# Convolution tiles kept as sums and differences of neighbours along the width, between three global convolutions and a Haar layer

## The chip, the cores and the metric

One core of one Trainium2 chip runs the whole program. The metric is device time in microseconds, the median of several runs. The core has a matrix engine (TensorE, in profiles PE, with its weight loads as PEld), a vector engine (VectorE, DVE), an activation engine (ScalarE, ACT), GpSimd (POOL) and a queue engine (SyncE, SP). The engines run side by side, each takes its own instructions in order, and they meet through semaphores. SBUF is the working memory with 128 partitions, PSUM the memory that matmuls write, DRAM the memory outside; DMA queues, here issued by SP and ACT, move data between DRAM and SBUF.

## What is computed

The input x has 4 images of 64 channels of 256 x 256, all in float32. Four layers follow each other:

```python
x = conv(x, L0); x = conv(x, L1); x = haar_mix(x, L2); x = conv(x, L3)

def conv(x, ...):                      # once per layer, filters hx, hy [256, 64] from a small network
    k = hx[:, None, :] * hy[None, :, :]            # separable kernel of channel c
    y = causal_2d_convolution(x, k)                # along height and width, cut to 256 x 256
    return y + x * bias[:, None, None]

def haar_mix(x, v, conv_w, tau):
    f1 = haar2d(x)                                 # full Haar transform along width and height
    f4 = einsum('bchw,oc->bohw', f1 * v[i], conv_w[i])          # for i = 0, 1, summed after
    f5 = sign(f4) * relu(abs(f4) - tau[i])                      # the soft threshold
    return haar2d_inverse(sum of f5) + x
```

The convolution is separable and causal, so the kernel does it as two products with Toeplitz matrices, one along the height and one along the width. The first step of the Haar transform along the width takes the sum and the difference of each pair of neighbouring columns, and the last step of the inverse makes the pair out of sum and difference again.

## The kernel before, in words

**A tile** is one channel of one image, 128 partitions x 2 x 256: row p of the upper and of the lower half. `toeplitz` (L249) loads a tile t of 128 x 2 x 256 from a short padded filter row in DRAM (`pads`), with overlapping reads: t[:, 0] is the band along the height, t[:, 1] the one along the width. `contract` (L258) is one product: four matmuls, each of which the page counts as two records. `first` (L264) multiplies a tile with the height band (PSUM tile pa) and ScalarE copies the product to SBUF (a, L275); this leaves it transposed. `second` (L279) multiplies a with the width band (PSUM tile py), which puts it back, and VectorE adds tile times bias (L292) into the result.

**Stages.** For each image b: `convolutions` (L322) loads x and runs layers 0 and 1 for each channel: stages load, a0, y0, a1, y1. Stage pairs (L335) then makes the sums and differences of neighbours of y1 with two VectorE operations, into the rings sums (4 channels) and sd (8 channels), and keep stores both in DRAM. Further levels of the width transform follow on VectorE and POOL (L344), two fp32r copies of the result (ACT L369, VectorE L374), the transform along the height as one matmul with a Haar matrix (pz, L381), and a store (coef). `mixing` (L425) runs 64 groups: load f, matmul with the channel weights (px, L449), scale (VectorE L468 and ACT L473), size and sign (ACT L477, L480), threshold and product (VectorE L484, L488), and a sum into the large tile z (L494). `inverse` (L517) takes z back: levels in place (VectorE L299, L300), copy of a channel (ACT L534), matmuls pw (L541, L542), for the first 16 channels a further product pu (L548 to L555), and join (L560): r, which is the kept sums and differences, times 0.5 plus the PSUM result gives t (L563), and two more operations (L566, L567) make neighbours out of its sums and differences, tile u. Then layer 3 runs on u (stages a3, y3) and the result is stored (out). For the first three images every third channel is put off: its u goes to DRAM (late), and `convolution` (L614) runs layer 3 on it beside the mixing of the last image.

**Order.** Every stage of every unit gets a time in ticks: the start of its unit plus an entry of `PLACE` (L26). The events are sorted by it (L680) and emitted in this order, and the tile framework sets the order of the instructions on each engine from it, places tiles into buffers and puts in all waits. A tick of the mixing is one group with, for images 1 to 3, about 0.9 channels of convolution; a tick of the inverse is one channel. Tiles come from rings by tag: y (5 buffers) holds y0 and u, in (3) holds x and the reloaded u, res (1) holds y1 and t, co (3) holds the result of layer 3 and the coefficients before their store; the six buffers of toep hold Toeplitz tiles.

**Start.** `filters` (L169) computes the filters of each layer from the small network on 128 partitions (64 for the height, 64 for the width) and stores them with `end` (L206) into pads, one store on ACT's queue, one on SP's; the first Toeplitz load waits for both. Dummy matmuls (`occupy`, L161) run on TensorE meanwhile.

Of the kernel before, what the change touches and what calls it, by code (L numbers as in the profile page):

```python
# [9 lines left out]
F32 = mybir.dt.float32  # L10
F32R = mybir.dt.float32r
AF = mybir.ActivationFunctionType
ALU = mybir.AluOpType
# [3 lines left out]
B, C, S, EMB, ORD = 4, 64, 256, 33, 64  # L17
P = 128
ROW = S + P

GT = 4
BUFS = {"res": 1, "y": 5, "co": 3}

N_ACT = (12, 12, 12, 8)

PLACE = {  # L26
    "load": 0.714,
    "a0": 1.643,
    "a0 copy": 1.643,
    "y0": 2.571,  # L30
# [2 lines left out]
    "a1 copy": 3.5,  # L33
    "y1": 4.429,
    "y1 sum": 4.429,
    "pairs": 4.639,
    "keep": 4.929,
    "levels": 0.73,
    "split": 0.734,
# [22 lines left out]
    "a3 copy": 2.471,  # L62
    "y3": 3.542,
    "y3 sum": 3.542,
    "out": 4.537,
    "level": 0.6,
    "l load": 0.316,
    "l a3": 1.855,
    "l a3 copy": 1.855,
    "l y3": 2.783,  # L70
    "l y3 sum": 2.783,
    "l out": 4.4,
    "l mix load": -0.977,
    "l mix": 0.21,
    "l scaled": 0.583,
# [22 lines left out]
def conv_seq_kernel(ctx, tc, x, fz, fw, bias, decay, haar, haar_row, factors, vt, taut, wmix, out):  # L98
# [14 lines left out]
    nc = tc.nc  # L113
# [27 lines left out]
    keep = [dram.tile([C, P, 2, 2, P], F32, name=f"keep{b}") for b in range(B)]  # L141
    coef = [dram.tile([2, C, P, S], F32, name=f"coef{b}") for b in range(B)]
    scales = dram.tile([S // 4 // GT, P, 2, GT, 16], F32, name="scales")
    pads = [dram.tile([C, 2, ROW], F32, name=f"pad{layer}") for layer in range(3)]
    late = dram.tile([B, C, P, 2, S], F32, name="late")


# [21 lines left out]
    def filters(layer, queue, done, behind=None):  # L169

        fz_sb, fw_sb = part(S + P, EMB), part(3 * P + 4)
        fb = part(3)
        par = 3 * P
        st = {}

        def load():
            nc.sync.dma_start(fz_sb, fz[layer])
            queue.dma_start(fw_sb, fw[layer])

            nc.vector.tensor_scalar(fb, fw_sb[:, par : par + 3], fw_sb[:, par + 3 : par + 4], None, ALU.mult)  # L180

        def begin(n):
            ps = bank(f"fp{layer}_{n}").rearrange("p m s -> p (m s)")[:, :S]
            if n == 0:
                nc.tensor.matmul(ps, fz_sb[:, S:], fz_sb[:, :S], start=True, stop=True)
            else:
                nc.tensor.matmul(ps, fw_sb[:, (n - 1) * P : n * P], st["h"], start=True, stop=True)
            u, k = st["u"], st["k"] = part(S), part(S)
            nc.scalar.activation(u, ps, AF.Identity, bias=fb[:, n : n + 1], scale=fw_sb[:, par + 3 : par + 4])

            first = nc.vector.tensor_scalar(k, u, INV_2PI, MAGIC, ALU.mult, ALU.add)
            if behind is not None:
                tc.add_manual_dep(first.ins, behind[n].ins.name, order, reason="the first layer goes first")
            nc.vector.tensor_scalar(k, k, -MAGIC, None, ALU.add)

        def finish(n):
            u, k, h = st["u"], st["k"], part(S)
            for c in (C1, C2):
                step = nc.vector.scalar_tensor_tensor(u, k, -c, u, ALU.mult, ALU.add)
                if n == 2 and behind is not None:  # L200
                    tc.add_manual_dep(step.ins, behind["out"].ins.name, order, reason="the first layer goes first")
            done[n] = nc.vector.tensor_scalar(u, u, PI_IN, -PI_IN, ALU.min, ALU.max)
            nc.scalar.activation(h, u, AF.Sin)
            st["h"] = h

        def end():  # L206
            ps = bank(f"fo{layer}").rearrange("p m s -> p (m s)")[:, :S]
            nc.tensor.matmul(ps, fw_sb[:, 2 * P : 3 * P], st["h"], start=True, stop=True)
            f = part(ROW)
            nc.vector.memset(f[:, S:], 0.0)  # L210
            done["out"] = nc.vector.scalar_tensor_tensor(f[:, :S], ps, dsb[:, S:], dsb[:, :S], ALU.mult, ALU.mult)
            for axis, queue in enumerate((nc.scalar, nc.sync)):
                queue.dma_start(pads[layer][:, axis, :], f[axis * C : (axis + 1) * C])
            st["f"] = f

        steps = [(lambda n=n, do=do: do(n)) for n in range(3) for do in (begin, finish)]
        return [load, *steps, end]
# [31 lines left out]
    def toeplitz(layer, c, name):  # L249

        t = tp.tile([P, 2, S], F32, name=name, tag="toep")
        nc.sync.dma_start(t, ap(pads[layer], c * 2 * ROW, [[1, P], [ROW, 2], [1, S]]))
        return t

    def bank(name):
        return psm.tile([P, 2, S], F32, name=name, tag="mm")

    def contract(ps, src, t):  # L258

# [19 lines left out]
    def second(b, st, key, layer, res, new, tag, ahead=None):  # L279


        def product(c):
            s = st[c]
            if ahead is not None:
                s[ahead] = toeplitz(ahead, c, f"t{ahead}_{b}_{c}")
            s["p" + new] = bank(f"p{new}_{b}_{c}")
            contract(s["p" + new], s[key], s[layer][:, 1, :])

        def residual(c):
            s = st[c]  # L290
            y = io.tile([P, 2, S], F32, name=f"{new}_{b}_{c}", tag=tag, bufs=BUFS[tag])
            nc.vector.scalar_tensor_tensor(y, s[res], bsb[:, layer, c : c + 1], s["p" + new], ALU.mult, ALU.add)  # L292
            s[new] = y

        return [product, residual]

    def halve(even, odd):

        nc.vector.tensor_sub(odd, even, odd)  # L299
        nc.vector.scalar_tensor_tensor(even, even, 2.0, odd, ALU.mult, ALU.subtract)  # L300

    def level(n, chunk, begin=0, count=None):

        count = n if count is None else count
        v = z.rearrange("p n s x c -> p n s (x c)")[:, chunk].rearrange("p (j e s) x -> p j e s x", e=2, s=P // 2 // n)
        halve(v[:, begin : begin + count, 0, 0, :], v[:, begin : begin + count, 1, 0, :])

    def butterfly():

# [12 lines left out]
    def convolutions(b, ticks, in_parts=(), border=None):  # L322


        st = {}
# [2 lines left out]
            return tick if border is None or tick < border or n < C // 4 - 2 else border + 3 * (tick - border)  # L328

        def load(c):  # L330
            xt = io.tile([P, 2, S], F32, name=f"x_{b}_{c}", tag="in", bufs=3)
            nc.sync.dma_start(xt, x[b, c].rearrange("(k p) w -> p k w", p=P))
            st[c] = {"x": xt, 0: toeplitz(0, c, f"t0_{b}_{c}")}

        def pairs(c):  # L335
            v = st.pop(c)["y1"].rearrange("p k (w e) -> p k w e", e=2)
            nc.vector.tensor_add(sums[:, c % 4], v[:, :, :, 0], v[:, :, :, 1])
            nc.vector.tensor_sub(sd[:, c % 8, 1], v[:, :, :, 0], v[:, :, :, 1])

        def store(c):  # L340
            nc.sync.dma_start(keep[b][c, :, 0], sums[:, c % 4])
# [48 lines left out]
        def away(c):  # L390
# [3 lines left out]
            nc.sync.dma_start(coef[b][:, c].rearrange("k p w -> p k w"), t)  # L394

        work = zip(
            ("load", "a0", "a0 copy", "y0", "y0 sum", "a1", "a1 copy", "y1", "y1 sum", "pairs", "keep"),
            [
                load,
                *first(b, st, "x", 0, "a0"),  # L400
                *second(b, st, "a0", 0, "x", "y0", "y", ahead=1),
                *first(b, st, "y0", 1, "a1"),
                *second(b, st, "a1", 1, "y0", "y1", "res"),
                pairs,
                store,
            ],
        )
# [109 lines left out]
    def inverse(b, start, put_off):  # L517
# [41 lines left out]

        def join(c):  # L560
            ps = st[c]["pw"]
            t = io.tile([P, 2, 2, P], F32, name=f"t_{b}_{c}", tag="res", bufs=BUFS["res"])
            nc.vector.scalar_tensor_tensor(t, st[c]["r"], 0.5, ps, ALU.mult, ALU.add)  # L563
            u = io.tile([P, 2, S], F32, name=f"u_{b}_{c}", tag="y", bufs=BUFS["y"])
            v = u.rearrange("p m (w e) -> p m w e", e=2)
            nc.vector.tensor_add(v[:, :, :, 0], t[:, 0], t[:, 1])  # L566
            nc.vector.tensor_sub(v[:, :, :, 1], t[:, 0], t[:, 1])  # L567
            st[c]["u"] = u

        def aside(c):  # L570
            nc.scalar.dma_start(late[b, c], st.pop(c)["u"])
# [17 lines left out]
        for c in range(C):  # L589
# [8 lines left out]
            if c in put_off:  # L598
                at(turn + PLACE["aside"], aside, c)
            else:  # L600
                shift = (0.0, 0.0)
                if put_off:
                    shift = ((-0.27, -0.342), (0.23, 0.158))[c % 3]
                for name, stage in zip(("a3", "a3 copy", "y3", "y3 sum", "out"), last(b, st)):
                    at(turn + PLACE[name] + shift[name[0] != "a"], stage, c)

    def last(b, st, queue=nc.scalar):
        return [
            *first(b, st, "u", 2, "a3"),
            *second(b, st, "a3", 2, "u", "y3", "co"),  # L610
            lambda c: queue.dma_start(out[b, c].rearrange("(k p) w -> p k w", p=P), st.pop(c)["y3"]),
        ]

    def convolution(which, ticks):  # L614

        for (b, c), tick in zip(which, ticks):
            st = {}

            def load(c, b=b, st=st):
                u = io.tile([P, 2, S], F32, name=f"v_{b}_{c}", tag="in", bufs=3)  # L620
                nc.sync.dma_start(u, late[b, c])
                st[c] = {"u": u, 2: toeplitz(2, c, f"t2_{b}_{c}")}

            for name, stage in zip(("l load", "l a3", "l a3 copy", "l y3", "l y3 sum", "l out"), [load, *last(b, st, nc.sync)]):
                at(tick + PLACE[name], stage, c)
# [168 lines left out]
```

## Time and profile before

| | |
|---|---|
| median of 3 runs | 2874.51 us (2872.78 to 2877.79) |
| profiled execution, its own time | 2874.07 us |
| its span, first to last instruction | 2872.3 us |
| granted TensorE clock, mean | 0.999 |
| ScalarE, VectorE and POOL busy, first row of their kind | ACT 72%, DVE 87%, POOL 12% |
| DMA, mean over the span | 226 GB/s |
| Toeplitz loads (t<-pad) | 768 of 256 KB, 4.1 us from issue to landing |
| x loads | 256 of 256 KB, 3.7 us |
| result stores from ACT's queue | 193 of 256 KB, 4.3 us |

The first matmul of a convolution starts at 25.17 us, after the filters. The stages of the span, read from the rows of each: convolutions of image 0 alone until about 420 us; mixing of image 0 with convolutions of image 1 until 840; the inverse of image 0 until 1080; the same pair for image 1 (mixing until 1500, inverse until 1740) and image 2 (2160, 2340); mixing of image 3 beside the channels that were put off until about 2640; the inverse of image 3 until the end.

Rows of instructions are read like this: line of the program, engine, operation, output<-inputs, output shape<-input shape, and how often. The times of a timeline row are its start and its duration. A duration is longer than what the instruction takes from its engine, since the next one starts before it ends; so a cost is read from start to start where the engine has no gap.

### The profile page before, as it was taken

What the parts mean: (1) busy time and instruction counts of PE and PEld (TensorE: products, weight loads), DVE (VectorE), ACT (ScalarE), POOL (GpSimd) and SP (SyncE); (2) the same over time, 40 slices, a digit from 0 to 9 for tenths busy, and PEclk for the clock granted to TensorE, in tenths of its full rate; (3) what the DMA queues carried; (4) which work ended last, traced back from release to release, by engine and by line L of the source; (5) the groups of instructions that cost most, each with busy time, mean ns of one, the idle gap of its engine ahead of it and who ended that gap; (6) DMA issues with size and microseconds to landing.
All of it is one profiled execution on the core that took longest, in us unless ns stands there. A gap on an engine that the chain in (4) does not pass through costs nothing. (4 is left out here: it accounts for less than half of the span.)

```text
span 2872.3 us, 52434 instructions
## 1 busy us (share of the span) xinstructions
PE 2827.1 (98%) x16592; PEld 2555.6 (89%) x16592; DVE 2494.9 (87%) x4255; ACT 2080.3 (72%) x4950; POOL 334.4 (12%) x644
## 2 busy tenths in 40 slices
PE   9999999999999999999999999999999999999999
PEld 7899998898888898998898998998898998888998
DVE  4655558999999779999999779999999779999985
ACT  2333338999995558998985658999995659998554
POOL 0111111121121001221221001121121000000000
PEclk9999999999999999999999999999999999999999
DMA  6878787776667986777777986777777988787786
GB/s 182 249 231 230 232 232 227 207 208 204 205 209 213 289 254 198 214 213 214 209 207 236 299 255 196 213 214 216 208 208 235 297 266 235 229 238 212 224 241 201
DMA packets 599367, 649.77 MB, mean 226 GB/s; under 512 B 48465, under 2 KB 517044, under 8 KB 598964
## 3 DMA queue, kind: packets, MB, share of 16 engines
q1 hardware_dynamic: 536996, 578.61, 68.9%
q10 hardware_dynamic: 62096, 67.82, 6.7%
q8 instruction: 134, 2.20, 0.3%
q14 instruction: 141, 1.16, 0.1%
HBM read 426.77 MB, written 219.48 MB: 225 GB/s over the span
## 5 line engine op out<-in xcount | busy, mean ns | idle before, releaser
L261 PE MATMUL py<-t,a 128*128 128x256 f32 x3072 | 922.5, 382 | 9.5 <-ACT a L275 8.7
L275 ACT COPY a<-pa 128x512 f32<-128x512 f32 x768 | 478.8, 623 | 498.6 <-PE pa L262 455.2
L473 ACT ACTIVATE f<-px,vt 128x64 f32<-128x64 f32 x2816 | 610.5, 367 | 101.6 <-DVE f L468 101.1
L262 PEld LDWEIGHTS py<-t,a 128*128 128x128 f32 x3072 | 583.4, 190 | 79.3
L262 PE MATMUL py<-t,a 128*128 128x128 f32 x3072 | 590.0, 274 | 0.0
L261 PEld LDWEIGHTS py<-t,a 128*128 128x128 f32 x3072 | 497.3, 191 | 51.2 <-ACT a L275 19.0
L449 PE MATMUL px<-wb,f 128*128 128x256 f32 x2048 | 487.6, 380 | 7.6 <-ACT f L473 7.6
L449 PEld LDWEIGHTS px<-wb,f 128*128 128x128 f32 x2048 | 369.0, 190 | 50.0 <-ACT f L473 10.5
L351 POOL TENSOR_TENSOR sd<-less 128x128 f32<-128x128 f32 (+4 forms) x320 | 190.8, 596 | 1858.7 <-DVE less L350 1519.9
L534 ACT COPY zc<-z 128x512 f32<-128x512 f32 x256 | 282.1, 1105 | 108.1 <-PE pw L542 99.0
L484 DVE TENSOR_TENSOR mag<-mag,vt 128x1024 f32<-128x1024 f32 x256 | 316.6, 1237 | 12.3 <-ACT mag L477 11.5
L488 DVE SCALAR_TENSOR_TENSOR mag<-mag,f 128x1024 f32<-128x1024 f32 x256 | 316.6, 1238 | 0.0
L261 PE MATMUL pa<-t,y 128*128 128x256 f32 x1024 | 309.1, 384 | 6.8 <-DVE y L292 5.2
L261 PE MATMUL pa<-t,x 128*128 128x256 f32 x1024 | 305.9, 381 | 0.5 <-DMA t<-pad 0.5
L477 ACT ACTIVATE mag<-f 128x1024 f32<-128x1024 f32 x256 | 295.7, 1155 | 2.8 <-DVE z L494 0.4
L374 DVE TENSOR_TENSOR sp<-sd,sp 128x512 fp32r<-128x512 f32 x256 | 179.8, 702 | 129.3 <-ACT sp L369 128.2
L480 ACT ACTIVATE f<-f 128x1024 f32<-128x1024 f32 x256 | 285.8, 1116 | 3.5
L261 PE MATMUL pa<-t,u 128*128 128x256 f32 x772 | 233.2, 384 | 6.5 <-ACT w L548 2.8
L292 DVE SCALAR_TENSOR_TENSOR y<-x,bsb,py 128x512 f32<-128x512 f32 x256 | 190.9, 746 | 41.9 <-PE py L262 41.0
L262 PEld LDWEIGHTS pa<-t,x 128*128 128x128 f32 x1024 | 194.6, 190 | 26.3
L262 PEld LDWEIGHTS pa<-t,y 128*128 128x128 f32 x1024 | 194.5, 190 | 26.3
L292 DVE SCALAR_TENSOR_TENSOR y<-y,bsb,py 128x512 f32<-128x512 f32 x256 | 190.7, 745 | 26.0 <-PE py L262 25.6
(73 smaller groups left out, 4412.3 us busy)
## 6 DMA issues: line engine op xcount, KB each, us to landing
t<-pad SPq DMA_DIRECT2D x768, 256.0 KB, 4.1
x<-in_x SPq DMA_DIRECT2D x256, 256.0 KB, 3.7
coef<-co SPq DMA_DIRECT2D x256, 256.0 KB, 3.2
f<-coef SPq DMA_DIRECT2D x256, 256.0 KB, 3.2
r<-keep SPq DMA_DIRECT2D x256, 256.0 KB, 4.1
out_y<-y ACTq DMA_DIRECT2D x193, 256.0 KB, 4.3
keep<-sums SPq DMA_DIRECT2D x256, 128.0 KB, 2.8
keep<-sd SPq DMA_DIRECT2D x256, 128.0 KB, 2.8
```

What stands on the lines that cost most here:

```text
L261: nc.tensor.matmul(ps[:, m, :], src[:, 0, m * P : (m + 1) * P], t[:, ::-1], start=True, stop=False)
L262: nc.tensor.matmul(ps[:, m, P:], src[:, 1, m * P : (m + 1) * P], t[:, : P - 1 : -1], start=False, stop=True)
L275: nc.scalar.copy(a, s["p" + new])
L292: nc.vector.scalar_tensor_tensor(y, s[res], bsb[:, layer, c : c + 1], s["p" + new], ALU.mult, ALU.add)
L351: engine.tensor_tensor(t[:, :, :, half:length], v[..., 0], v[..., 1], ALU.subtract)
L449: nc.tensor.matmul(ps[:, q, h, :], f[:, q, h * P : (h + 1) * P], wb.rearrange("p r n -> p (r n)"), start=True, stop=True,)
L473: nc.scalar.mul(f4[:, j], px[:, j], scale(g, 0)[:, j : j + 1])
L477: nc.scalar.activation(mag, st[g]["f4"], AF.Abs)
L480: nc.scalar.activation(st[g]["f4"], st[g]["f4"], AF.Sign)
L484: nc.vector.tensor_sub(mag, mag, over(g, 1, 16))
L488: nc.vector.scalar_tensor_tensor(mag, mag, 0.0, st[g]["f4"], ALU.max, ALU.mult)
L534: nc.scalar.copy(a.rearrange("p h k i -> p (h k) i"), z[:, c // 16, :, :, c % 16].rearrange("p i x -> p x i"))
```

## The change

Tiles of layers 0, 1 and 3 are kept in another form along the width: in place of columns 2n and 2n + 1 they hold their sum and their difference, alternating. The width band is brought into this form too, so that a product with it takes alternating sums and differences to alternating sums and differences. The height products are as they were.

- x is turned into this form by two POOL operations of 128 x 256 (`butterflies`, stage pairs, now between load and the Toeplitz load, which is a stage of its own, bands). The x load moves from 0.714 to -1.0 ticks.
- y1 needs no tile of its own and no pairs after it: its residual is two VectorE operations of half a tile that write straight into sums and sd.
- join makes u with two VectorE operations of half a tile out of r and the PSUM result. Channels that are put off still get plain neighbours, by the three operations of before, since their layer 3 runs on plain tiles with plain bands (pads[3]).
- After layer 3 a new stage, neighbours, turns the result back with two POOL operations (two VectorE ones for the very last channel), and out, which stores it, moves from 4.537 to 5.2. The late channels' store (l out) moves from 4.4 to 4.8.
- `end` stores four padded rows per channel in place of two: the height filter twice, once shifted by one, and two width rows in the new form, which six short VectorE operations on 64 partitions make. A Toeplitz load reads them with three levels: 64 steps of two elements, 4 rows, 256 elements. The first two channels of each image load height and width bands separately (EARLY).
- The rings in and res are gone, y has nine buffers.

```diff
-BUFS = {"res": 1, "y": 5, "co": 3}
+BUFS = {"y": 9, "co": 3}
...
-            for axis, queue in enumerate((nc.scalar, nc.sync)):
-                queue.dma_start(pads[layer][:, axis, :], f[axis * C : (axis + 1) * C])
+            for i, queue in enumerate((nc.sync, nc.scalar)):
+                queue.dma_start(pads[layer][:, i, 0, : ROW - 1], f[:C, i : i + ROW - 1])
+            g0, g1, g2 = (f[C:, i : i + S : 2] for i in range(3))
...
+            nc.vector.tensor_add(sums, g0, g2)
+            nc.vector.tensor_sub(less, g0, g2)
+            nc.vector.scalar_tensor_tensor(w[:, 0, :P, 1], sums, 0.5, g1, ALU.mult, ALU.add)
+            nc.vector.tensor_scalar(w[:, 0, :P, 0], less, -0.5, None, ALU.mult)
+            nc.vector.tensor_scalar(w[:, 1, :P, 1], less, 0.5, None, ALU.mult)
+            nc.vector.scalar_tensor_tensor(w[:, 1, :P, 0], sums, -0.5, g1, ALU.mult, ALU.add)
+            nc.sync.dma_start(pads[layer][:, :, 1, :], w.rearrange("p i n o -> p i (n o)"))
...
-        nc.sync.dma_start(t, ap(pads[layer], c * 2 * ROW, [[1, P], [ROW, 2], [1, S]]))
+        if layer == 0 and c < EARLY:
+            for axis in range(2):
+                nc.sync.dma_start(
+                    t[:, axis], ap(pads[layer], (c * 4 + axis) * ROW, [[2, P // 2], [2 * ROW, 2], [1, S]])
+                )
+        else:
+            nc.sync.dma_start(t, ap(pads[layer], c * 4 * ROW, [[2, P // 2], [ROW, 4], [1, S]]))
...
+    def butterflies(engine, t, name):
+
+        new = io.tile([P, 2, S], F32, name=name, tag="y", bufs=BUFS["y"])
+        v, w = (a.rearrange("p k (n e) -> p k n e", e=2) for a in (t, new))
+        engine.tensor_add(w[:, :, :, 0], v[:, :, :, 0], v[:, :, :, 1])
+        engine.tensor_sub(w[:, :, :, 1], v[:, :, :, 0], v[:, :, :, 1])
+        return new
...
+            if new == "y1":
+                scale = bsb[:, layer, c : c + 1]
+                v, ps = (a.rearrange("p k (n e) -> p k n e", e=2) for a in (s[res], s["p" + new]))
+                for e, to in enumerate((sums[:, c % 4], sd[:, c % 8, 1])):
+                    nc.vector.scalar_tensor_tensor(to, v[..., e], scale, ps[..., e], ALU.mult, ALU.add)
...
         def pairs(c):
-            v = st.pop(c)["y1"].rearrange("p k (w e) -> p k w e", e=2)
-            nc.vector.tensor_add(sums[:, c % 4], v[:, :, :, 0], v[:, :, :, 1])
-            nc.vector.tensor_sub(sd[:, c % 8, 1], v[:, :, :, 0], v[:, :, :, 1])
+            st[c]["x"] = butterflies(nc.gpsimd, st[c]["x"], f"xb_{b}_{c}")
...
-            nc.vector.tensor_add(v[:, :, :, 0], t[:, 0], t[:, 1])
-            nc.vector.tensor_sub(v[:, :, :, 1], t[:, 0], t[:, 1])
...
+            for e in range(2):
+                behind[0] = nc.vector.scalar_tensor_tensor(
+                    v[:, :, :, e], st[c]["r"][:, e], 0.5, ps[:, e], ALU.mult, ALU.add
+                )
...
+        def neighbours(c):
+            engine = nc.vector if b + 1 == B and c + 1 == C else nc.gpsimd
+            st[c]["y3"] = butterflies(engine, st[c]["y3"], f"out_{b}_{c}")
```

## The prediction

> **What bounds the kernel now.** First the page's busy shares, then busy time per engine in stretches cut at the stages, then single rows and timelines.
>
> ```profile
> PE 2827.1 (98%) x16592; PEld 2555.6 (89%) x16592; DVE 2494.9 (87%) x4255; ACT 2080.3 (72%) x4950; POOL 334.4 (12%) x644
> ```
>
> TensorE is busy for all but 45.2 us of the 2872.3 us span, and the change takes no matmul from it: the instruction lists of the two programs have the same 8,874 matmuls. So only waiting can go.
>
> ```profile
> 60.00:420.00 360.00, 358.45 (x2131) 326.07 (x2130) 213.30 (x392) 136.58 (x252) 45.61 (x150) 1.00 0.81 235
> 420.00:840.00 420.00, 415.74 (x2308) 371.20 (x2307) 401.48 (x678) 382.47 (x1093) 82.71 (x134) 1.00 0.71 211
> 840.00:1080.00 240.00, 230.44 (x1458) 209.88 (x1457) 201.71 (x364) 141.58 (x217) 12.17 (x27) 0.99 0.81 247
> 1080.00:1500.00 420.00, 417.79 (x2342) 376.07 (x2342) 413.72 (x682) 378.55 (x1073) 88.03 (x140) 1.00 0.72 209
> 2340.00:2640.00 300.00, 290.85 (x1598) 260.37 (x1596) 291.83 (x434) 275.62 (x711) 0.00 (x0) 1.00 0.78 232
> ```
>
> (PE, PEld, DVE, ACT, POOL; clock; DMA share; GB/s.) The first row is convolutions alone: VectorE has 40% to spare. In mixing with convolutions beside it (rows 2 and 4) VectorE is busy 96 to 99%, so TensorE and VectorE bound it together.
>
> Matmul ends are modelled, so short stalls hide inside "busy". I laid every PE start against the pace of undisturbed stretches (128x256 record 0.217 us, 128x128 0.110, 128x512 0.274). The excess is 85 us: 10 in the first 60 us; 0 in 60 to 420; 8.9, 7.5 and 5.4 in the three mixing stages (420-840, 1080-1500, 1740-2160); 15.7, 5.6 and 5.5 in the three returns (840-1080, 1500-1740, 2160-2340); 21.7 in the late mixing (2340-2640); 5.0 after it. The waits in the return's worst part:
>
> ```profile
> PE pw L541 <- ACT zc L534: 2.0, 1, 2.0
> PE pw L541 <- DVE w L549: 1.5, 1, 1.5
> PE pa L261 <- DVE y L292: 1.4, 1, 1.4
> ```
>
> There VectorE has no gap from 865 to 905 us; what it has not got to is what TensorE waits for.
>
> **The change, part by part.** *y1 and its pairs.* VectorE issues follow each other closer than their durations: in the timelines a 128x256 operation frees it after 0.34 us, 128x512 after 0.60 (L292, with its bias column, 0.66), PSUM source or not. Before: 0.66 + 2 x 0.34 = 1.34 us a tile. After: two 128x256 operations with a bias column; no such row, so between 0.33 (half of L292) and 0.40 (0.34 + 0.06); I take 0.38 and get 0.76. Saved 0.57 us x 256.
> *join.* L563 0.60 + L566 and L567 0.68 become 2 x 0.34: saved 0.60 us for the 193 tiles not put off. In all 0.57 x 256 + 0.60 x 193 = 262 us of VectorE. In 60 to 420 it is worth nothing; in a mixing stage 64 x 0.57 = 36 us, in a return 43 x 0.60 = 26 us and the tail of the convolutions.
>
> *New POOL work.* 512 butterflies of x and 384 of the output. Nearest rows, undisturbed in the first stage: POOL takes 0.45 us for 128x128 and 0.29 for 128x64, so about 0.77 for 128x256: 690 us more on an engine now busy 334. Whether it hurts is a matter of SBUF access:
>
> ```profile
> 1186.56 3.33 POOL L351 TENSOR_TENSOR sd<-less 128x128 f32<-128x128 f32 x1 [22.75 <-ACT sp L369]
> 1189.85 0.76 POOL L350 TENSOR_TENSOR less<-less 128x128 f32<-128x128 f32 x2
> 1190.57 2.60 POOL L351 TENSOR_TENSOR sd<-less 128x64 f32<-128x64 f32 x1
> ```
> ```profile
> 1187.26 1.22 DVE L488 SCALAR_TENSOR_TENSOR mag<-mag,f 128x1024 f32<-128x1024 f32 x1
> 1188.40 1.22 DVE L484 TENSOR_TENSOR mag<-mag,vt 128x1024 f32<-128x1024 f32 x1
> 1189.53 0.75 DVE L292 SCALAR_TENSOR_TENSOR y<-x,bsb,py 128x512 f32<-128x512 f32 x1
> 1190.19 0.42 DVE L468 TENSOR_TENSOR f<-px,vt 128x256 f32<-128x256 f32 x1
> 1190.53 0.76 DVE L494 TENSOR_TENSOR z<-mag 128x256 f32<-128x256 f32 x2
> ```
>
> The POOL operation that needs 0.45 us sits for 3.33 while VectorE runs operations with two SBUF tensors, and finishes once L292, which reads PSUM, starts; the next slips in behind it, and L494 starts as if nothing had been there. Over the whole trace a VectorE operation that meets POOL frees VectorE 0.00 to 0.08 us later in the median. The Trainium skill (SBUF — State Buffer, "SBUF: two separate sides") speaks against the change: the port pair is an exclusive lock held for the whole instruction, and the loser blocks fully. By that rule alone each of a convolution's two POOL operations could cost VectorE its 0.77 us: 1.54 - 0.57 = +0.97 us x 192 tiles in mixing, 186 us slower. By the row VectorE's back-to-back work wins and POOL starts in the shadow of a PSUM operation; what remains is the part longer than that shadow: about 0.1 us behind L292 (0.66), 0 behind the two y1 halves (0.76), 0.44 behind L468 (0.33). I take 0.2 us: 0.4 a convolution, so mixing nets 0.17 us a tile (11 us a stage); ends 0 and 0.44. In a return the shadows are joins and y3 sums, 0.66 and longer: 0.1, net 0.4 a tile.
>
> *What that is worth.* Mixing excess 21.8: half, 11 us. Returns: the first loses 15.7 with VectorE full for 95 us; its relief there is some 8 tiles x 0.57 + 17 joins x 0.60 = 14.8 less 4 of POOL, and I take 10; of the other two, 3 each. After the late mixing (64 joins at 0.60): 3 of 5. The late mixing itself (VectorE 97%) has neither pairs nor joins: nothing of its 21.7. Sum 30 us.
>
> *Costs on the path.* POOL now lies between the x load and the first matmul, 0.1 to 1.643 ticks: 1.54 x 6.8 us = 10.5 us in mixing (tick from 8 mix records and 0.89 of a convolution, 34 records, at the pace above). Two operations with waits like those shown take 3 to 6 us; behind a levels chain (8.2 us here) they can be late. Between 0 and 16 us in all; I take 6. Behind a late xb on POOL stand only other butterflies and levels; TensorE, in order, waits with them. The output's DMA moves from 4.537 to 5.2 on ACT's queue and now waits for POOL; behind it stand ACT's copies. It has 1.66 ticks, over 4 us: nothing in the median, counted in the 6.
> Start: six short VectorE operations on 64 partitions per layer, and on SP the pad stores for the new bands and for layer 1 stand before parts of tiles 0 and 1. The first tile's first half (issued at 21.79, used at 25.17) keeps its place; the second half and layer 1's first tile slip 1 to 3 us against less than 1 of slack: +2 us (0 to 4).
> End: the last tile gets two VectorE operations behind L292: +0.8 us.
> Tile loads: as many bytes and 1 KB rows, with 64 instead of 128 outer steps. They run at DMA share 0.81 in the first stage, where they are some 40% of the bytes; a quarter longer would give 0.9, so TensorE hides it; beyond half longer it would not. The x load goes to -1.0 on SP's queue; the nine shared buffers replace 5 + 3 + 1; by the table's times x, xb and y0 hold one for 1.1, 2.5 and 1.9 ticks, at 0.89 tiles a tick five in all: no wait, except where convolutions' tail meets the return (8 to 9), in the 6 above.
> Net 30 - 6 - 2 - 0.8 = 21 us. The profiled execution took 2874.07 us (span 2872.3, and 1.8 around it), near the median 2874.51: **2853 us**.
>
> **Rivals.** A, as above, 0.62; its own range 2834 to 2867 (relief 18 to 42, costs 3 to 16).
> B, the gain is given back: POOL's 0.285 us an operation cancels the saving in mixing, late butterflies eat the returns: 2870, from 2863 to 2879, 0.14. For it: TensorE has only 45 us of visible idle, much of it out of reach.
> C, slower by the lock: POOL starts mostly in the short 0.33 us shadow or wins against two-SBUF work. At 0.44 an operation, 0.88 - 0.57 = +0.31 us x 192 = 60 us on a full VectorE, less 16 from the returns, plus 9 of costs: 2927. It decides above 0.285 us an operation. Against it: the small delays in the trace; for it: no POOL operation there is longer than 0.45 unblocked. 0.13.
> D, slower by late xb: 1 us behind each of the 48 levels chains in mixing: 2853 - 6 + 48 = 2895; it decides from 0.56 us a chain. For it: 8.2 + 2 x 3.3 is over 10.5. 0.11.
>
> **How the numbers follow.** About 0.2% (5.7 us) is what this kernel's measurement can tell from no change. Faster: A but for 0.01, and 0.05 of B: 0.66. Same: 0.01 of A, 0.07 of B, 0.01 of D: 0.09. Slower: the rest, 0.25. The range goes from A's lower end over B to the nearer part of D: 2834 to 2890 leaves out C (0.13) and over half of D (0.06).
>
> **What would show it.** Right: VectorE some 240 to 260 us less busy; 420-840 and 1080-1500 below 96%; TensorE's idle in 840-1080 down from 9.6 to 3 us or less; 2340-2640's twin unchanged. Wrong: TensorE waiting for xb from POOL (D); L484, L488 or L494 longer on average than now (C); ACT waiting at the output's DMA; tile loads far over 4.1 us to landing with TensorE waiting in the first stage.

## The result, and the profile after

The changed kernel takes **2943.68 us** (median of 4 runs, 2939.34 to 2947.12) against 2875.69 before: 1.0236 times as long, 95% interval 1.0219 to 1.0254. That is 68.0 us slower, where 21 us faster was forecast. First the engines' busy time of the changed kernel:

```profile
span 2941.6 us, 53014 instructions
## 1 busy us (share of the span) xinstructions
PE 2850.6 (97%) x16592; PEld 2555.7 (87%) x16592; DVE 2334.5 (79%) x3829; ACT 2070.8 (70%) x4950; POOL 1067.6 (36%) x1540
```

TensorE has the same instructions and more gaps: 91 us of the span in place of 45.2. VectorE lost 160 us of work, not 240 to 260. Where the time went is read from the stages. A mixing stage is cut from its first matmul (px) to the first matmul of its last group, a return from there to the next mixing; "to mix 0" is all before the first of them, and return 3 ends with the last matmul:

| us | to mix 0 | mix 0 | return 0 | mix 1 | return 1 | mix 2 | return 2 | mix 3 | return 3 |
|---|---|---|---|---|---|---|---|---|---|
| before | 443.9 | 397.1 | 219.4 | 433.3 | 215.5 | 433.2 | 212.3 | 269.5 | 243.8 |
| after | 447.3 | 409.3 | 222.4 | 448.0 | 226.2 | 448.8 | 221.3 | 271.0 | 242.0 |
| difference | +3.4 | +12.2 | +3.0 | +14.7 | +10.7 | +15.6 | +9.0 | +1.5 | -1.8 |

So 42.5 us came in the three mixing stages that run beside convolutions, and 22.7 in the three returns. The stretches of the changed kernel that answer to the second and fourth of before (columns PE, PEld, DVE, ACT, POOL, clock, DMA share, GB/s):

```profile
420.00:840.00 420.00, 408.06 (x2246) 360.92 (x2245) 400.42 (x622) 369.06 (x1047) 181.70 (x233) 1.00 0.67 206
1080.00:1500.00 420.00, 409.44 (x2284) 366.32 (x2283) 393.83 (x612) 359.95 (x1023) 196.50 (x229) 1.00 0.65 202
```

VectorE is busy less than before in both (401.48 and 413.72), as wanted, and yet TensorE is busy 8 us less in each: an engine with more room, in a stage that became longer. What TensorE and ScalarE wait for (us in all, times, longest), first in the changed kernel, then before:

```profile
ACT a L309 <- POOL out L289: 56.0, 61, 2.7
...
PE pa L295 <- DVE y L333: 37.8, 52, 2.1
...
PE py L295 <- ACT a L309: 20.2, 47, 1.3
```
```profile
PE py L261 <- ACT a L275: 8.7, 15, 1.4
PE pa L261 <- DVE y L292: 5.2, 11, 1.4
```

TensorE's first matmul of layer 1 (pa from y) waits 37.8 us for VectorE's y0, where it waited 5.2 us before; the second product waits 20.2 us for ScalarE's copy a, 8.7 before. Nearly all of the wait for y0 lies in the three mixing stages: TensorE's idle time before pa from y is 11.2, 12.9 and 13.4 us there, and was 1.2, 1.6 and 1.6. ScalarE stands 56.0 us at a row that did not exist: the result that POOL turns back, in front of its store. One such wait of TensorE, in the timeline of the second mixing stage:

```profile
1189.23 0.69 DVE L421 TENSOR_TENSOR sp<-sd,sp 128x512 fp32r<-128x512 f32 x1 [1.17 <-ACT sp L416]
1189.62 0.78 POOL L288 TENSOR_TENSOR xb<-x 128x256 f32<-128x256 f32 x1 [4.36 <-DMA x<-in_x]
...
1190.25 1.23 DVE L532 TENSOR_TENSOR mag<-mag,vt 128x1024 f32<-128x1024 f32 x1
1190.36 1.59 POOL L289 TENSOR_TENSOR xb<-x 128x256 f32<-128x256 f32 x1
...
1191.59 1.44 DVE L536 SCALAR_TENSOR_TENSOR mag<-mag,f 128x1024 f32<-128x1024 f32 x1
...
1192.96 0.41 DVE L516 TENSOR_TENSOR f<-px,vt 128x256 f32<-128x256 f32 x1
1193.29 0.41 DVE L542 TENSOR_TENSOR z<-mag 128x256 f32<-128x256 f32 x1
...
1193.62 0.74 DVE L333 SCALAR_TENSOR_TENSOR y<-xb,bsb,py 128x512 f32<-128x512 f32 x1
...
1194.42 0.70 PE L295 MATMUL pa<-t,y 128*128 128x256 f32 x2 [0.98 <-DVE y L333]
```

POOL's second butterfly, 0.61 us where nothing meets it, takes 1.59 beside L532 and L536; L536 starts at 1191.59, 1.34 after L532 where 1.13 is usual, and takes 1.44 where 1.23 was usual. VectorE had idled 1.17 us shortly before (for ScalarE's sp), so it had the room, but not when it was needed; y0 comes late, and TensorE, in order, stands 0.98 us. The same matmul, counted in TensorE's order, starts without a wait in the kernel before (1173.15 us).

### The profile page after: what moved, and what is told of

The parts are those of the page before. It is cut to its first block, busy times and chain, and to the rows that moved or that the text cites. A ratio compares the mean times of both kernels' runs of the same rounds, so it can differ in the third digit from the quotient of the medians.

```text
span 2941.6 us, 53014 instructions
## 1 busy us (share of the span) xinstructions
PE 2850.6 (97%) x16592; PEld 2555.7 (87%) x16592; DVE 2334.5 (79%) x3829; ACT 2070.8 (70%) x4950; POOL 1067.6 (36%) x1540
## 5 line engine op out<-in xcount | busy, mean ns | idle before, releaser
L295 PE MATMUL py<-t,a 128*128 128x256 f32 x3072 | 926.9, 383 | 20.9 <-ACT a L309 20.2
L295 PEld LDWEIGHTS py<-t,a 128*128 128x128 f32 x3072 | 497.4, 191 | 71.1 <-ACT a L309 37.8
L288 POOL TENSOR_TENSOR xb<-x 128x256 f32<-128x256 f32 x256 | 228.2, 892 | 655.4 <-DMA x<-in_x 525.2
L288 POOL TENSOR_TENSOR out<-y 128x256 f32<-128x256 f32 x192 | 136.0, 708 | 831.8 <-DVE y L333 511.3
L295 PE MATMUL pa<-t,y 128*128 128x256 f32 x1024 | 313.2, 388 | 42.0 <-DVE y L333 37.8
L398 POOL TENSOR_TENSOR sd<-less 128x128 f32<-128x128 f32 (+4 forms) x320 | 204.4, 639 | 371.7 <-DVE less L397 357.7
L333 DVE SCALAR_TENSOR_TENSOR y<-u,bsb,py 128x512 f32<-128x512 f32 x193 | 143.8, 746 | 246.1 <-issue 186.2
L421 DVE TENSOR_TENSOR sp<-sd,sp 128x512 fp32r<-128x512 f32 x256 | 192.7, 753 | 184.3 <-ACT sp L416 182.4
L532 DVE TENSOR_TENSOR mag<-mag,vt 128x1024 f32<-128x1024 f32 x256 | 323.5, 1264 | 19.4 <-ACT mag L525 19.0
L536 DVE SCALAR_TENSOR_TENSOR mag<-mag,f 128x1024 f32<-128x1024 f32 x256 | 325.3, 1271 | 2.1
L295 PE MATMUL pa<-t,xb 128*128 128x256 f32 x1024 | 305.8, 380 | 0.0
L289 POOL TENSOR_TENSOR xb<-x 128x256 f32<-128x256 f32 x256 | 253.9, 992 | 0.0
L333 DVE SCALAR_TENSOR_TENSOR y<-xb,bsb,py 128x512 f32<-128x512 f32 x256 | 189.3, 739 | 80.2 <-PE py L296 35.8
```

What stands on the lines that cost most here:

```text
L288: engine.tensor_add(w[:, :, :, 0], v[:, :, :, 0], v[:, :, :, 1])
L295: nc.tensor.matmul(ps[:, m, :], src[:, 0, m * P : (m + 1) * P], t[:, ::-1], start=True, stop=False)
L532: nc.vector.tensor_sub(mag, mag, over(g, 1, 16))
L536: nc.vector.scalar_tensor_tensor(mag, mag, 0.0, st[g]["f4"], ALU.max, ALU.mult)
```

## The experiments

Each ratio is against executions of the kernel before taken beside it, with its 95% interval. The edits are against the changed kernel, if not said otherwise.

**Whose work is it?** *e1_no_x* leaves out the butterflies of x, *e2_no_out* the neighbours of the result, *e3_neither* both.

```diff
 def pairs(c):
-    st[c]["x"] = butterflies(nc.gpsimd, st[c]["x"], f"xb_{b}_{c}")
+    pass                                                       # e1, e3
...
-            *([neighbours] if queue is nc.scalar else []),
+            *([lambda c: None] if queue is nc.scalar else []),   # e2, e3
```

> The changed kernel without the POOL butterflies of x: layer 0 takes x as loaded, so layers 0 to 3 compute something else; 512 POOL operations are left out, everything else is there. POOL theory (the POOL work, by the port it shares with VectorE or by its lateness, makes the mixing stages slow): the three mixing stages lose their 12 to 16 us each, some 2895 us. Order theory (the instruction order on VectorE and the half-tile residuals make it slow, POOL is innocent): 2935 us or more.

> The changed kernel without the POOL stage neighbours: the result is stored as sums and differences, straight from the tile that VectorE wrote; 384 POOL operations are left out. POOL theory: only the returns gain, the second and third get back their 10 us each, some 2915 us. Order theory: 2935 us or more.

> Both left out: POOL does only the levels that it did before. POOL theory: what is left is a kernel whose VectorE has 260 us less to do than before, 2850 us, some 25 below the kernel before. Order theory: still some 2930 us.

Measured: e1 2897.41 us, 1.0073 [1.0058, 1.0088]; e2 2899.64, 1.0082 [1.0067, 1.0097]; e3 2853.71, 0.9921 [0.9906, 0.9935]. All the loss is POOL's new work: 90 us, 46 for x and 44 for the result, and they add. All else in the change (VectorE's saving, order, bands, rings, start) is worth -22.7 us. In e3 mixing takes 393.4, 433.3 and 433.4 us and the returns 206.2, 211.7 and 209.6. Its second mixing stage beside that of before:

```profile
1080.00:1480.00 400.00, 398.01 (x2233) 358.35 (x2233) 394.00 (x651) 359.44 (x1013) 82.74 (x130) 1.00 0.71 209
```
```profile
1080.00:1480.00 400.00, 398.08 (x2231) 358.68 (x2230) 374.78 (x599) 359.45 (x1019) 84.62 (x130) 1.00 0.68 210
```

(Before, then e3.) VectorE is relieved of 19 us, and TensorE is as busy as before: 99.5% in both. The stage keeps its 433.3 us. Its 2418 matmul records, at the paces that the prediction gives (0.217, 0.110 and 0.274 us), fill 433.1 of them. There was nothing to gain in it; TensorE alone set its length.

**Length or reading?** *e4_narrow* makes all butterflies 8 columns wide and in place (most of the transform is left out), so that the chain still runs over POOL but shortly.

```diff
-        new = io.tile([P, 2, S], F32, name=name, tag="y", bufs=BUFS["y"])
-        v, w = (a.rearrange("p k (n e) -> p k n e", e=2) for a in (t, new))
...
+        v = t.rearrange("p k (n e) -> p k n e", e=2)[:, :, :4]
+        engine.tensor_add(v[:, :, :, 0], v[:, :, :, 0], v[:, :, :, 1])
+        engine.tensor_sub(v[:, :, :, 1], v[:, :, :, 0], v[:, :, :, 1])
+        return t
```

> All 896 POOL butterflies are there, in the same places and with the same waits, but 128x8 in place of 128x256, in the tile itself: most of the transform is left out, the chain from x over POOL to TensorE and from VectorE over POOL to the store stays. If the length of POOL's operations (the shared port) is the cause: near the kernel with neither, 2850 to 2865 us. If it is that TensorE, ACT and VectorE wait for POOL's place in the chain: 2910 us or more. Order theory: 2930 us.

Measured 2889.09, 1.0044 [1.0028, 1.0061]; mixing 393.9, 434.2 and 434.1. The step over POOL as such costs mixing nothing; its size does. (In all it is 35 us above e3, more than expected; most of that lies in the returns, 216.0, 222.9 and 212.5, where ScalarE still stands 54.3 us for POOL before the copies a.) But size is two things: the time for which a tile is held back, and the reading of SBUF beside VectorE. *e8_beside* keeps e4's narrow chain and adds the two whole operations beside it: they read x and write a tile that nobody reads, with eight buffers in y to make room.

```diff
+        if name[0] == "x":
+            junk = io.tile([P, 2, S], F32, name=f"junk_{name}", tag="junk", bufs=1)
+            v, w = (a.rearrange("p k (n e) -> p k n e", e=2) for a in (t, junk))
+            engine.tensor_add(w[:, :, :, 0], v[:, :, :, 0], v[:, :, :, 1])
+            engine.tensor_sub(w[:, :, :, 1], v[:, :, :, 0], v[:, :, :, 1])
```

> The narrow kernel (128x8 butterflies in place, most of the transform left out) with two full 128x256 POOL operations per x tile added behind the narrow ones: they read x and write a tile that nobody reads, so TensorE does not wait for them. Shared port: the mixing stages are at 405 to 410 and 445 to 450 us as in the changed kernel, 2925 to 2935 us. Late butterflies: mixing stays at 394 and 434, about 2890 us.

Measured 2941.13, 1.0229 [1.0211, 1.0247]; mixing 406.4, 453.5 and 451.3, with TensorE never waiting for x from POOL. Its twin *e9_late* was to hold the tiles back by two fills of a tile that nobody reads:

> The narrow kernel with two 128x512 memsets on POOL ahead of each narrow butterfly of x: POOL is busy and x later ready, by as much as the memsets take, but they read nothing in SBUF. Shared port (by reads): mixing at 394 and 434 us, about 2890 us. Late butterflies: mixing longer, towards 448, by as much as the memsets are as long as the full butterflies (0.61 us alone).

Measured 2930.54, 1.0190 [1.0175, 1.0205], and of no use for the question: nothing tied the fills to the tiles, so all 512 ran in the first 360 us; the stretch to mix 0 took 493.4 us, 46 more than in after, mixing no more than in e4 (393.3, 433.5 and 434.0). It does show that eight buffers in y, as in e8, cost mixing nothing. *e13_memset* mends it: four fills go into the x tile itself, ahead of e4's narrow butterflies, and overwrite what they cover.

```diff
+        if name[0] == "x":
+            for _ in range(4):
+                engine.memset(t[:, :, 8:], 0.0)
```

> The butterflies of x are cut to 8 columns in place (both x and result, as in e4_narrow), and ahead of those of x POOL fills the rest of the x tile with zeros four times: about 4 x 0.51 = 2.04 us of POOL work per tile that must run between the x load and the first matmul, as long as the two real butterflies took in mixing (2 x 1.04), but writes only and reads no SBUF. The image's content is left out. Port theory (reading two SBUF operands on POOL beside VectorE costs VectorE): mixing as with narrow butterflies, 394, 434 and 434 us, about 2890 us, 1.005. Rival (a long stage on POOL ahead of the matmul makes TensorE late): mixing 406 to 409 and 445 to 450, about 2935.

Measured 2892.39, 1.0054 [1.0037, 1.0071]; mixing 394.0, 434.0 and 433.2. This settles it: the time on POOL is not the cause. The stretch 1100 to 1500 us, first of after, then of e13:

```profile
1100.00:1500.00 400.00, 389.44 (x2169) 348.08 (x2168) 378.51 (x582) 347.68 (x989) 186.77 (x219) 1.00 0.65 202
```
```profile
1100.00:1500.00 400.00, 397.26 (x2223) 356.99 (x2222) 375.43 (x600) 360.81 (x1019) 234.25 (x451) 1.00 0.69 211
```

In e13 POOL is busy longer (234 against 187 us), and ahead of the same matmul, yet TensorE is 99.3% busy and mixing as short as before. TensorE's idle time before pa from y in the three mixing stages is 2.0, 2.5 and 2.0 us in e13, 10.2, 15.2 and 14.7 in e8; and the matmul of the timeline, which stands 0.98 us in after, stands 0.69 in e8 and not at all in e3 and e13. What differs is the form of POOL's work, and how it and VectorE's rows meet. First after, then e13 (count, busy us, mean ns, idle before):

```profile
L289 POOL TENSOR_TENSOR xb<-x 128x256 f32<-128x256 f32 x49 | 55.6, 1135 | 0.0
...
L536 DVE SCALAR_TENSOR_TENSOR mag<-mag,f 128x1024 f32<-128x1024 f32 x56 | 72.5, 1295 | 0.9
L532 DVE TENSOR_TENSOR mag<-mag,vt 128x1024 f32<-128x1024 f32 x56 | 71.6, 1279 | 5.8 <-ACT mag L525 5.8
L542 DVE TENSOR_TENSOR z<-mag 128x256 f32<-128x256 f32 x111 | 48.0, 463 | 0.2
L333 DVE SCALAR_TENSOR_TENSOR y<-xb,bsb,py 128x512 f32<-128x512 f32 x51 | 37.5, 736 | 0.0
L421 DVE TENSOR_TENSOR sp<-sd,sp 128x512 fp32r<-128x512 f32 x46 | 36.4, 791 | 11.9 <-ACT sp L416 11.3
```
```profile
L288 POOL MEMSET x<- 128x496 f32 x208 | 104.4, 512 | 85.8 <-DMA x<-in_x 71.1 <-PE px L499 4.4 <-PE pa L298 3.7
...
L534 DVE TENSOR_TENSOR mag<-mag,vt 128x1024 f32<-128x1024 f32 x59 | 72.1, 1222 | 5.4 <-ACT mag L527 5.4
L538 DVE SCALAR_TENSOR_TENSOR mag<-mag,f 128x1024 f32<-128x1024 f32 x58 | 70.6, 1218 | 1.1 <-ACT f L530 0.4
L544 DVE TENSOR_TENSOR z<-mag 128x256 f32<-128x256 f32 x118 | 46.6, 426 | 0.3
L335 DVE SCALAR_TENSOR_TENSOR y<-x,bsb,py 128x512 f32<-128x512 f32 x52 | 38.3, 737 | 0.0
L423 DVE TENSOR_TENSOR sp<-sd,sp 128x512 fp32r<-128x512 f32 x50 | 34.7, 695 | 7.7 <-ACT sp L418 6.5
```

The operations of VectorE with SBUF sources alone (mag, z, sp) are 37 to 96 ns longer when POOL reads beside them; the one that reads PSUM (y) is not. POOL's fills take the 512 ns they need, its butterfly 1135 where 610 would do. Read from start to start where VectorE has no gap, against the median of the same row in e3, VectorE's operations from 1090 to 1490 us take 19.8 us more in after and 1.4 in e13. For some 98 butterflies that is 0.19 us each.

**Which layers?** *e6_first_layers* has layers 0 and 1 in the new form and layer 3 plain (three VectorE operations in join, no neighbours, the stores at their old times).

```diff
-            if c in put_off:
+            if True:
                 t = io.tile(...)
...
-                st[c][2] = toeplitz(2, c, f"t2_{b}_{c}")
+                st[c][2] = toeplitz(3, c, f"t2_{b}_{c}")
```

> Half of the change alone: layers 0 and 1 in the new form, layer 3 plain (every join by three operations, no neighbours on POOL, the store from ACT straight behind VectorE at its old time). If the two POOL uses cost separately, the mixing stages stay at 409, 448 and 449 us and the returns are like those of the kernel before (219, 215, 212): some 2920 us. If the returns' loss came from layers 0 and 1 too (nine shared buffers, earlier x loads), the returns stay over 220.

Measured 2900.85, 1.0089 [1.0074, 1.0104]: mixing 407.9, 448.1 and 449.5 as in after, returns 207.5, 213.9 and 209.1. The two losses belong to two separate parts. It is 19 us faster than expected, since its returns are shorter than before: the first by 11.9 us, with layer 3 plain. So most of what e3 gains there (13.2) came with layers 0 and 1 and their rings and places, not with the shorter join.

**Is it the load on VectorE?** *e11_on_vector* makes every butterfly on VectorE (`nc.gpsimd` becomes `nc.vector` in pairs and neighbours).

> The changed kernel with every pair of butterflies (x and result) on VectorE in place of POOL. VectorE then has 0.68 - 0.57 = 0.11 us more per convolution and 0.68 - 0.60 = 0.08 more per return tile than in the kernel before, but POOL no more than before. Port theory: mixing 397 to 401, 433 to 440, 433 to 440, returns 220 to 226, 216 to 222, 212 to 220 (the store on ACT still waits for VectorE): 2880 to 2910 us. If load on VectorE were what mixing pays for, it has more here than in the changed kernel by 0.68 a tile: mixing beyond 448 and over 2960 us.

Measured 2906.37, 1.0100 [1.0085, 1.0115]: mixing 395.5, 437.0 and 436.8. VectorE is then busy 2527.1 us in all, 193 more than in after, and mixing is 11 to 14 us shorter. A busy VectorE costs less here than a disturbed one.

**The returns.** *e7_out_sp* leaves the neighbours on POOL and issues the store from SP:

```diff
-            lambda c: queue.dma_start(out[b, c].rearrange("(k p) w -> p k w", p=P), st.pop(c)["y3"]),
+            lambda c: nc.sync.dma_start(out[b, c].rearrange("(k p) w -> p k w", p=P), st.pop(c)["y3"]),
```

> The changed kernel with the store of the result issued by SP in place of ACT, nothing else. If ACT, in order, stands at the store until POOL is done and TensorE then waits for ACT's copy, the returns come down from 222, 226 and 221 us to about 210 each, some 2910 us in all; the mixing stages stay. If it is VectorE that waits for the tile that POOL has not yet read, or the port: 2935 us or more. SP may then hold up Toeplitz loads itself, which would show as TensorE waiting for t.

Measured 2922.42, 1.0162 [1.0147, 1.0177], 21 us less than after: returns 214.1, 218.8 and 213.4. ScalarE no longer waits at POOL's result (56.0 us in after), and TensorE's wait for the copy a falls from 20.2 to 7.8 us: behind the store, in ScalarE's order, stood the copies that TensorE needs. On top of e7, *e16_sp_narrow* cuts the result's neighbours to 8 columns in place, and *e17_sp_memset* puts two fills of the result tile ahead of these.

```diff
+        if name[0] == "o":
+            for _ in range(2):                                   # e17 only
+                engine.memset(t[:, :, 8:], 0.0)
+            v = t.rearrange("p k (n e) -> p k n e", e=2)[:, :, :4]
+            engine.tensor_add(v[:, :, :, 0], v[:, :, :, 0], v[:, :, :, 1])
+            engine.tensor_sub(v[:, :, :, 1], v[:, :, :, 0], v[:, :, :, 1])
+            return t
```

> The changed kernel with the store on SP as in e7_out_sp, and the neighbours of the result made for 8 columns only, in place (the rest stays sums and differences); x's butterflies whole. Mixing as in the changed kernel. With the store on SP and whole operations the returns were 214, 219 and 213; without any, on ACT, 206, 212 and 208. Both theories (POOL's reads; length in the chain): returns 207 to 209, 212 to 215, 208 to 210, about 2905 us. If neither, but the step over POOL as such: still 214, 219, 213 and 2922.

> As e16_sp_narrow, and POOL fills the rest of the result tile with zeros twice ahead of it, 2 x 0.51 us, so that POOL is in the chain for about as long as with the whole operations but reads nothing more. Reads theory (the port): returns as e16_sp_narrow, about 2905 us. Length theory (y3's buffer is held longer, VectorE waits for it): returns 214, 219, 213, about 2922 us.

Measured: e16 2910.56, 1.0120 [1.0103, 1.0136]; e17 2913.48, 1.0127 [1.0110, 1.0144]. The returns are 211.0, 215.8 and 212.1, and 211.3, 216.1 and 212.1: the fills cost them nothing, so POOL's time in the chain is not the cause here either. (The profiled execution of e17 was its slowest, 2918.28 us, with 453.1 in the second mixing stage, which the fills do not explain.) In e7 one VectorE row of the returns is long: the last operation of the plain join of a channel that is put off, which has two SBUF sources. From 860 to 1070 us, e7, then e16:

```profile
L617 DVE TENSOR_TENSOR u<-t 128x256 f32<-128x256 f32 x20 | 15.4, 772 | 0.0
```
```profile
L622 DVE TENSOR_TENSOR u<-t 128x256 f32<-128x256 f32 x21 | 8.8, 419 | 0.0
```

That is 0.35 us an operation, 7 to 8 us in each return, and it goes with POOL's whole operations. But the 12 us between e7 and e16 are not all shown to be POOL's reads: the returns account for 7.4 of them (3.1, 3.0 and 1.3), and e16 and e17 also turn the result in its own tile, so that it takes no buffer of the shared ring of nine; no run parts the two. The last 11 us (e16 to e2) remain with the step over POOL and SP as such, which I did not split further. So the result's 44 us are 21 (ScalarE in order at the store), 12 (whole operations in a tile of their own, POOL's reads among it) and 11.

**Is there a form that gains?** *e5_last_layer* has layers 0 and 1 plain (bands, pairs and the place of the x load as before) and layer 3 alone in the new form; *e10_last_sp* is e5 with the store on SP; *e12_first_return* is e10 with layer 3 plain for images 1 and 2, their stores on ACT at the old place.

```diff
 def pairs(c):                                    # e5, e10, e12: on VectorE, after y1
-    st[c]["x"] = butterflies(nc.gpsimd, st[c]["x"], f"xb_{b}_{c}")
+    v = st.pop(c)["y1"].rearrange("p k (w e) -> p k w e", e=2)
+    nc.vector.tensor_add(sums[:, c % 4], v[:, :, :, 0], v[:, :, :, 1])
+    nc.vector.tensor_sub(sd[:, c % 8, 1], v[:, :, :, 0], v[:, :, :, 1])
...
-            if c in put_off:
+            if c in put_off or not new_form(b):          # e12: new_form(b) is b in (0, 3)
```

> Layers 0 and 1 as in the kernel before (plain tiles, plain bands, pairs of y1 on VectorE), layer 3 alone in the new form, with its 193 pairs of neighbour operations on POOL and the store on ACT. Port theory (POOL's butterflies of x delay the chain in mixing, its neighbours the returns): mixing stages as before, 397, 433 and 433 us, returns as with the neighbours alone, 220, 224 and 222: about 2898 us, 1.008 of the time before. If instead the new order or the new bands made mixing longer, 409, 448 and 449 and 2935.

> Layer 3 alone in the new form as in e5_last_layer, and the result store on SP's queue in place of ACT's. If ACT standing at the store costs 21 us of the returns as the run with the store moved said: returns about 214, 219 and 213, in all 2875 to 2879 us, no better than before. If SP's queue now holds back loads of mixing or of the returns: nearer 2898.

> As e10_last_sp, but layer 3 of images 1 and 2 plain as in the kernel before, with their stores on ACT at the old place: the new form is left only where VectorE was full before (first return) and behind the late mixing. Theory: returns 214, 216 and 212, last inverse 241 to 242 against 243.8: 5 + 2 us less than before, about 2868 us, 0.9975. If the new form gains nothing there either: 2875 or more.

Measured: e5 2934.03, 1.0193 [1.0172, 1.0215]; e10 2914.94, 1.0129 [1.0114, 1.0144]; e12 2902.12, 1.0085 [1.0067, 1.0102]. All three are some 35 us above what their parts should give. Mixing behaved (399.3, 435.1 and 434.6 in e5); 20 us sat in the first convolutions (464.4 to mix 0). In all three, x, y1 and t shared the one ring of nine with y0 and u. *e15_rings_all* and *e14_rings* are e10 and e12 with the rings of before:

```diff
-BUFS = {"y": 9, "co": 3}
+BUFS = {"in": 3, "res": 1, "y": 5, "co": 3}
```

> As e12_first_return (new form only in layer 3 of images 0 and 3, store on SP there), with rings of buffers as before: x and the turned result in one of 3, y1 and t in one of 1, y0 and u in one of 5. Ring theory (x loads waited for a shared buffer that another stage still held): first convolutions back from 435.5 to 419, mixing from 401, 435 and 436 to 397, 433 and 433, first return from 222.8 to 214: 2902 - 17 - 9 - 9 = 2867 us, 0.997. If the rings are not the cause: 2895 to 2905.

> As e10_last_sp (new form in layer 3 of all four images, store on SP), with the same rings as before. Ring theory: first convolutions 419, mixing 397, 433 and 433, returns 214, 219 and 213, last inverse 242: 2873 us, 0.999. If the rings are not the cause: 2905 to 2915.

Measured: e15 2876.93, 1.0004 [0.9996, 1.0013]; e14 **2874.31, 0.9989 [0.9980, 0.9997]**. The rings were 38 and 28 us: to mix 0 took 445.4 us (e15) in place of 465.0 (e10), and the returns shrank as well. In these two some matmuls change sides between return 0 and mix 1, so the two are taken together: 647.9 us in e14 and 648.0 in e15, 652.7 before. e15 loses that again in the next pairs of stages (651.7 against 648.7, then 485.0 against 481.8). e14 beats both kernels, by 0.11% of before: a gain in the first return, where VectorE was full, and behind the late mixing (241.9 against 243.8), and nowhere else. It has the new form and the store on SP together in images 0 and 3; the store on SP alone was not run, so the gain is not shown to be the form's.

## Why the prediction was wrong, point by point

**VectorE's saving: right.** 262 us were forecast. With POOL's new work gone VectorE is busy 2240.4 us in e3, 254 less than before. In after 90 of these come back as longer operations (2334.5 against e13's 2244.7): 0.10 us for each of 896 butterflies on average.

**POOL's operation: right in size.** "About 0.77" was 0.61 undisturbed.

**The delay per operation: right.** I weighed the Trainium skill's page "SBUF — State Buffer", section "SBUF: two separate sides", an exclusive lock held for the whole instruction, against the row in which POOL waited, and took 0.2 us in mixing and 0.1 in returns. Measured: 0.19 in mixing, far from a whole butterfly. The section also says that only a POOL instruction that reads SBUF contends with a VectorE instruction of two SBUF inputs, not one that only writes; e13 and after agree (1.4 and 19.8 us of excess). So the rule's direction holds. My reading at the full price, a whole POOL operation lost to VectorE each time, does not: the two share the loss, VectorE by 0.19 us and POOL by some 0.4 to 0.5 (from 0.61 to 1.01 and 1.14). Whether the loser of a single meeting is blocked for the whole instruction, no run here tells.

**What mixing would make of it: the step that failed.** "0.4 a convolution, so mixing nets 0.17 us a tile (11 us a stage)" and "Mixing excess 21.8: half, 11 us" took VectorE's time as one account, in which a delay is paid from a saving. It is not. The saving was worth 3.7, 0 and 0 us (e3): at 433.3 us TensorE itself set the length, and VectorE's 96 to 99% busy were not a second bound. The excess of 21.8 does not stand either: at the same paces, with late starts set off against early ones, the three stages before held 4.5, 0.2 and 0.1 us. The delay was worth 45 us (after 409.3, 448.0 and 448.8, against 394.0, 434.0 and 433.2 in e13). It falls into single operations between a matmul and the next matmul that needs their result: TensorE's idle time before pa from y0 is 37.5 us in the three stages after and 6.5 in e13, 31 of the 45. The freed time lies elsewhere, in VectorE's waits for ScalarE (sp 2.4 to 11.9 us, mag 0.2 to 5.8 in the second mixing stage). How one engine's order carries the delay on to y0 I traced in one place only.

**The returns.** Relief of 10, 3 and 3 us was forecast; e3 shows 13.2, 3.8 and 2.7. Behind the late mixing 3 were forecast, 3.1 came. The late mixing itself, forecast unchanged, is 269.5 in e3. All of it was eaten: "It has 1.66 ticks, over 4 us: nothing in the median" was the second failed step. ScalarE stood at the store 61 times for 56.0 us, which cost 21; the step as such cost 11, and the whole operations 12. "Costs on the path ... I take 6" had a ceiling of 16; the result's store and step alone came to 32.

**Start and end.** +2 us were forecast for the start; the first matmul came 1.3 later and the first convolutions took 2.1 more (in e3 the whole stretch to mix 0 took 7.5 us more than before, which I did not follow). The tile loads did not suffer: 3.6 us to landing against 4.1.

**The rivals.** D (late xb) is out: TensorE never waits for xb, and holding the tile back by fills costs nothing. B, with 2863 to 2879, is out too. C had the right place, cause and sign, and a false threshold: it was to decide above 0.285 us an operation, where VectorE's account turns negative. It decided at 0.19, because no such account sets the time. Of the signs named beforehand, longer mag and z rows and ScalarE's waits at the store did show it. One sign for "right", VectorE below 96% in 420-840 and 1080-1500, came true as well (95.3 and 93.8%) while the kernel became slower.

## What to carry to other kernels

Work moved to POOL was not free beside VectorE, even though POOL had the time and nobody waited for it: what counted was its form, two operands read from SBUF while VectorE runs operations with two SBUF sources in a chain that the bounding engine waits for. Ask of a saving and of a delay separately what each is worth in its stage: the saving on an engine beside a TensorE that was 99.5% busy was worth nothing, and of the delay of 0.19 us for each of some 320 butterflies in mixing (61 us) 45 came out as time. And when a store comes to wait for one more engine, look at what stands behind it on the queue that issues it; moving it to a queue without compute took back 21 us with one word.

## What the runs showed of the hardware

- POOL writing zeros (0.51 us for 128 x 496, four in a row) did not slow VectorE, while POOL reading two operands for as long did: 1.4 against 19.8 us of excess in 400 us, at 104 and 105 us of POOL's time. The loss depends on the form of POOL's work, not on its time; reading and arithmetic were not parted.
- VectorE's operations with a PSUM source (y, 736 and 737 ns) stayed as they were; those with SBUF sources alone (mag, z, sp) grew by 37 to 96 ns on average.
- One shared ring of nine buffers for x, y0, y1, u and t cost 38 us against the same nine in three rings of 3, 1 and 5 (e10 and e15). Nothing else differs between the two programs; which of the tiles held the others up I did not follow.
